# Second layer by token pairs, banks emptied by ScalarE, and longer pauses in a four-block kernel on one Trainium2 core

## The chip, the cores and the metric

The kernel runs on 1 core of one Trainium2 chip. The metric is the device time of one execution in microseconds (us). Engines are named as in the profile: PE is TensorE's matmul, PEld its weight load, DVE is VectorE, ACT is ScalarE, POOL is GpSimd, SP is SyncE. A line such as L1104 is a line of the kernel before the change.

## What is computed

The input is x, 8 batches of 512 tokens of 256 features, in float32. Four blocks follow each other, each with a layer norm ahead of it and a residual add behind it:

```
x = x + attn_a(layernorm(x))     # 16 heads; softmax attention of the 307 "sparsest" queries
x = x + ffn(layernorm(x))        # 16 blocks of 64 hidden units, the 4 likeliest are kept
x = x + attn_b(layernorm(x))     # gated linear attention, then a SwiGLU layer
x = x + ffn(layernorm(x))        # the same FFN and weights again
```

`ffn` takes softmax(x @ router_w.T + router_b), keeps the top 4 of 16 blocks per token, and computes relu(x @ w1.T + b1), masked by block, times w2.T, plus b2.

`attn_b` works along an axis of only 8 steps (the batches) with 16 heads of 16 features: S = a * S + k (x) v, o = q S. The output o is normalised per head over its 16 features, multiplied by silu(x @ wog.T + bog), and taken through wo. The kernel does this without a scan: for two steps i and j that are d apart it forms the products q * k, sums them per head, and multiplies v by the sum, with the decay folded into k or q.

## The kernel before

The first attention runs first, up to about 556 us. The change touches nothing of it. What follows is worked in four slices of tokens, k = 0 to 3: slice k holds the 128 tokens k of every one of the 8 batches, so 8 token tiles of 128 tokens, in two groups g of 4 tiles (512 columns).

**The products of the FFN and of SwiGLU** are made by `group`. A feature tile f (of NF = 8) is first computed for the 512 columns of a group in a PSUM bank of pool `r_h` (4 banks; two products of 128x512 in float32, each of which the profile lists as two records). ACT empties the bank (L1148, L1165), DVE multiplies by the mask or by the other half (L1149, L1167). This is an *up* unit. The *down* unit of f (L1104) takes the four token tiles through the second layer and adds them up over f in two banks of pool `r_y`, two token tiles in each. A list named `waiting` holds a down unit back until LAGS = 4 later feature tiles have been computed. After the last f, `end` (L1098) adds each bank to the residual `xres` on DVE and so frees it for the next group.

**Everything else** of a slice, meaning the router (`route`) and the linear attention (`gla`), is a Python generator that yields after each small step. `between(units, pieces, n)` lays n such pieces evenly between the units. The stages behind the first attention are, in order, `routed_ffn(0..3)`, `swiglu(0..3)` and `last_ffn(0..3)`; the pieces of `gla(k)` are laid into the stages ahead of `swiglu(k)`, and `some(g[1], 51)` takes 51 pieces of slice 1 ahead into the stage before. GLA is the number of pieces that one slice counts for. `pause(n)` yields n times and does nothing, so PE's work goes on while DVE and POOL compute. A swiglu stage has 48 units, a routed stage 32.

**The small products** share the two banks of pool `r_l` (`bank_l`): the transpositions of `to_channels` (tile chT_ps), the projections (`project`, tile proj_ps), the transpositions of the attention's output (oT_ps) and its output product (gla_y).

**One slice of `gla`** goes as follows. Two halves m of 8 heads are handled one after the other by `heads(m)`. First come 8 projections, one per batch, each into one bank: ACT copies key, query and value out (L1243), DVE adds the bias bog to the gate's 128 columns (L1244). ACT then takes the Silu of the whole gate (L1290). Six steps of `weighed` follow with pauses between: a one-element copy on POOL (`hold`, L1085) makes a step wait for the newest FFN result, then DVE forms products (L1256), sums them (L1258) and multiplies by v (L1266); POOL multiplies keys by the decay (L1297) and adds results up (L1283, L1303). Then ACT squares the output (L1333), POOL multiplies it by the gate (L1334) and DVE sums the squares (L1335). After both halves ACT takes the root of the variances (L1342), DVE the reciprocal (L1343) and the multiplication of o[m] (L1346); PE transposes o (L1355), and ACT copies the transposed output (L1356).

**The order on an engine** is not the order of the code. The framework plans the queue of each engine when the program is built, by its own costs and by the order in the code among what it takes to be ready. Each engine then works its queue strictly in order.

Of the kernel before, what the change touches and what calls it, by code (L numbers as in the profile page):

```python
# [15 lines left out]
ALU = mybir.AluOpType  # L16
# [3 lines left out]
P = 128  # L20
NB = 8
# [4 lines left out]
NC2 = D // P  # L26
# [3 lines left out]
NF = DFF // P  # L30
# [14 lines left out]
def block_kernel(ctx: ExitStack, tc: tile.TileContext, t: dict, out: bass.AP):  # L45
    nc = tc.nc
# [64 lines left out]
    with ExitStack() as outer:  # L111
# [75 lines left out]
        with ExitStack() as inner:  # L187
# [554 lines left out]
            for n in range(len(steps) + LAG + 1):  # L742
# [3 lines left out]
                batch, i = divmod(n - LEAD, 16)  # L746
# [91 lines left out]
        with tc.tile_pool(name="a_tail", bufs=2) as tail:  # L838
# [5 lines left out]
            last = outC[5][0:1, 1, 0:1]  # L844
# [54 lines left out]
    def bank_y(name):  # L899
        return ps_y.tile([P, 512], F32, tag="y", name=name)  # L900

    def bank_l(name):
        return ps_l.tile([P, 512], F32, tag="l", name=name)
# [15 lines left out]
    def tokens(k, b, n=2):  # L919
        return xres[:, b : b + n, k, :]  # L920

    def pairs(y):
        return y.rearrange("p (b d) -> p b d", d=D)
# [24 lines left out]
    def to_channels(rows, dst, scale):  # L948

        for c in range(NC2):  # L950
            ps = bank_l("chT_ps")
            for i in range(G4):
                nc.tensor.transpose(ps[:, bass.ts(i, P)], rows[i][:, bass.ts(c, P)], ident)
            if scale is not None:
                nc.scalar.activation(dst[:, c, :], ps, AF.Copy, scale=scale[:, c : c + 1])
            elif c == 0:
                nc.vector.tensor_copy(dst[:, c, :], ps)
            else:
                nc.scalar.copy(dst[:, c, :], ps)
            yield  # L960
# [122 lines left out]
    def hold(dst):  # L1083

        nc.gpsimd.tensor_copy(dst, newest[0])  # L1085
# [4 lines left out]
    def group(k, g, ups, w, last=False):  # L1090


        h, y = [], []

        def end(i, n):
            b = G4 * g + i
            x = tokens(k, b, n)
            nc.vector.tensor_tensor(x, x, pairs(y[i // 2])[:, i % 2 : i % 2 + n], ALU.add)  # L1098
            newest[0] = xres[0:1, b, k, 0:1]
            if last:  # L1100
                nc.sync.dma_start(out=out_v[:, b : b + n, k, :], in_=x)

        def add(f, i):
            nc.tensor.matmul(  # L1104
                y[i // 2][:, bass.ts(i % 2, D)], h[f][:, bass.ts(i, P)], w[:, f, :],
                start=(f == 0 and i % 2 == 0), stop=(f == NF - 1 and i % 2 == 1),
                skip_group_check=True,
            )

        def down(f):  # L1110
            if f == 0:
                y.extend(bank_y("y_ps") for _ in range(2))
            if last and k == 3 and g == 1 and f >= NF - 2:
                if f == NF - 1:
                    for i in range(4):
                        for e in (f - 1, f):
                            add(e, i)
                        end(i, 1)
                return
            for i in range(4):  # L1120
                add(f, i)
            if f == NF - 1:
                for i in (0, 2):
                    end(i, 2)

        units = []
        for f in range(NF):
            units += [functools.partial(up, h, g, f) for up in ups]
            waiting.append(functools.partial(down, f))
            if len(waiting) > LAGS:  # L1130
                units.append(waiting.pop(0))
        return units
# [41 lines left out]
    def heads_of(x, axis="n"):  # L1174
        return x.rearrange(f"p {axis} (h d) -> p ({axis} h) d", d=DH)

    def gla(k):
# [18 lines left out]
        ps = bank_l("gh_ps")[:, 0 : 2 * P]  # L1196
# [14 lines left out]
        for us in ((1, 2, 3), (0,)):  # L1211
            ps = [bank_l("al_ps") for u in us]
# [21 lines left out]
        def project(made, gate, m, b):  # L1234

            ps = bank_l("proj_ps")
            for c in range(NC2):
                nc.tensor.matmul(  # L1238
                    ps, rT[b // G4][:, c, bass.ts(b % G4, P)], q_w[:, c, m],
                    start=(c == 0), stop=(c == NC2 - 1),  # L1240
                )
            half = ps.rearrange("p (x n) -> p x n", n=P)
            nc.scalar.copy(made[:, :, b, :], half[:, 0:3, :])  # L1243
            nc.vector.tensor_tensor(gate[:, b, :], half[:, 3, :], bog[:, m, :], ALU.add)  # L1244

        def weighed(parts):

# [28 lines left out]
        def heads(m):  # L1276


            def fours(x):
                return x.rearrange("p (u i) n -> p u i n", i=G4)  # L1280

            def add(dst, src):
                nc.gpsimd.tensor_tensor(dst, dst, src, ALU.add)  # L1283

            made = rest.tile([P, 3, NB, P], F32, tag="made", name="made")
            gate = rest.tile([P, NB, P], F32, tag="gate", name="gate", bufs=2)
            for b in range(NB):
                project(made, gate, m, b)
                yield
            nc.scalar.activation(gate, gate, AF.Silu)  # L1290
            key, q, v = (fours(made[:, i]) for i in range(3))
            a, out = fours(al[:, :, bass.ts(m, P)]), fours(o[m])

            def near(d):
                n = G4 - d
                if d > 0:
                    nc.gpsimd.tensor_tensor(  # L1297
                        key[:, :, 0:n, :], key[:, :, 0:n, :], a[:, :, d:, :], ALU.mult
                    )
                return q[:, :, d:, :], key[:, :, 0:n, :], v[:, :, 0:n, :]  # L1300

            pr = weighed([near(0)])[0]
            nc.gpsimd.tensor_copy(out, pr)  # L1303
            yield from pause(5)
            pr = weighed([near(1)])[0]
            add(out[:, :, 1:, :], pr)
            yield from pause(4)
            for d in (2, 3):
                pr = weighed([near(d)])[0]
                add(out[:, :, d:, :], pr)  # L1310
                yield from pause(4 - d // 3)
            nc.gpsimd.tensor_tensor(q[:, 1, 0, :], q[:, 1, 0, :], a[:, 1, 0, :], ALU.mult)
            nc.gpsimd.tensor_tensor(
                q[:, 1, 1:, :], q[:, 1, 1:, :], far[:, :, bass.ts(m, P)], ALU.mult
            )
            every = [P, 2, G4, P]
            for s in (0, 2):
                pr = weighed([(
                    q[:, 1].unsqueeze(1).to_broadcast(every),
                    key[:, 0, s : s + 2, :].unsqueeze(2).to_broadcast(every),  # L1320
                    v[:, 0, s : s + 2, :].unsqueeze(2).to_broadcast(every),
                )])[0]
                if s == 0:
                    for i in range(2):
                        add(out[:, 1], pr[:, i])
                else:

                    nc.vector.tensor_tensor(pr[:, 0], pr[:, 0], pr[:, 1], ALU.add)
                    nc.vector.tensor_tensor(out[:, 1], out[:, 1], pr[:, 0], ALU.add)
                yield from pause(5 + s)  # L1330
            sq = rest.tile([P, NB, P], F32, tag="pr", name="sq", bufs=2)
            hold(sq[0:1, 0, 0:1])
            nc.scalar.activation(sq, o[m], AF.Square)  # L1333
            nc.gpsimd.tensor_tensor(o[m], o[m], gate, ALU.mult)  # L1334
            nc.vector.tensor_reduce(var[:, m, :], heads_of(sq), AX.X, ALU.add)  # L1335
            yield
# [4 lines left out]
            yield from heads(m)  # L1341
        nc.scalar.activation(var, var, AF.Sqrt, bias=eps, scale=1.0 / DH)  # L1342
        nc.vector.reciprocal(var, var)  # L1343
        oT = rest.tile([P, 2, NC2, 512], F32, tag="made", name="oT")
        for m in range(NC2):
            nc.vector.tensor_tensor(  # L1346
                heads_of(o[m]), heads_of(o[m]),
                var[:, m, :].unsqueeze(2).to_broadcast([P, NB * P // DH, DH]), ALU.mult,
            )
            yield from pause(1 + m)  # L1350
        for g in range(2):
            for m in range(NC2):
                ps = bank_l("oT_ps")
                for i in range(G4):
                    nc.tensor.transpose(ps[:, bass.ts(i, P)], o[m][:, G4 * g + i, :], ident)  # L1355
                nc.scalar.copy(oT[:, g, m, :], ps)  # L1356
                yield
# [42 lines left out]
        ready["z", k] = zT  # L1400


    GLA = 97

    def chain(*gens):
        return itertools.chain(*gens)
# [1 line left out]
    def pause(n):  # L1408

        for _ in range(n):  # L1410
            yield
# [11 lines left out]
    bog = wpool.tile([P, NC2, P], F32, name="bog")  # L1423
# [7 lines left out]
    ps = bank_l("bog_ps")[:, 0:D]  # L1431
    nc.tensor.matmul(ps, ones, turned, start=True, stop=True)
    nc.vector.tensor_copy(bog.rearrange("p m n -> p (m n)"), ps)
    g = [gla(k) for k in range(4)]
# [17 lines left out]
    )  # L1452
    between(routed_ffn(3, (1, 3)), chain(g[0], some(g[1], 51)), GLA - 91 + 51)
    between(swiglu(0), chain(g[1], some(g[2], 36)), GLA - 51 + 36)
    between(swiglu(1), chain(g[2], some(g[3], 26)), GLA - 36 + 26)
    between(swiglu(2), chain(g[3], route(0, (2, 0))), GLA - 26 + ROUTE)
    resting.close()
# [107 lines left out]
```

## Time and profile before

| | |
|---|---|
| time, median of 3 runs | 1571.51 us (1569.48 to 1574.36) |
| profiled execution, its own time | 1567.76 us |
| its span, first to last instruction | 1566.0 us |
| mean granted TensorE clock | 0.983 |
| DVE busy, share of the span | 985.5 us, 63% |
| ACT busy | 735.3 us, 47% |
| POOL busy | 451.9 us, 29% |

A group's line reads: kernel line, engine, operation, output<-inputs, shape, count | busy us, mean ns | idle time of the engine just before it and what ended that. A line of waits reads: engine and line that waited <- engine and line that ended the wait: us in total, times, longest us. A line of windows gives, for a stretch from A to B in us, its length, then busy us and number of instructions of PE, PEld, DVE, ACT and POOL, then the granted clock of PE, the DMA share and GB/s. A line of the timeline gives start and duration in us, engine, line, operation, output<-input and count, and in brackets the idle time of the engine before it and what ended it. Neighbouring instructions of one line are merged.

### The profile page before, as it was taken

Reading aid. Unit: us, or ns where it says so; the run is one execution under the profiler, and the core shown is the slowest. Engines: PE = TensorE matmul, PEld = TensorE weight load, DVE = VectorE, ACT = ScalarE, POOL = GpSimd, SP = SyncE. Lnnn points to the kernel's source line nnn. Section 1 sums busy time; section 2 is a strip of 40 time slices with the busy share of each in tenths; the row PEclk is TensorE's granted clock in tenths of the full one; section 3 lists DMA queues with packets and bytes.
Section 4 is the critical chain, followed back from the end, with each engine's and each line's share of the span. In section 5 each row is a group of like instructions: output and inputs, shape, how many; then the busy total and the mean of one; then the engine's idle time right before and its main releaser. Section 6 shows DMA issues by size and latency. Waiting matters only on the chain.

```text
span 1566.0 us, 21950 instructions
## 1 busy us (share of the span) xinstructions
PE 1519.2 (97%) x8110; PEld 882.8 (56%) x8110; DVE 985.5 (63%) x2047; ACT 735.3 (47%) x1341; POOL 451.9 (29%) x547
## 2 busy tenths in 40 slices
PE   6899999999999999999999999999999999999999
PEld 2444444444444376655565556555555656788887
DVE  5878776776778983636773674457375733476654
ACT  3457777777766843452336216323613363232221
POOL 4743443433320151133341443224233221010000
PEclk8879999999999999999999999999999999999999
DMA  5302111111120051100000000000000010011110
GB/s 185 133 2 79 46 43 69 46 53 49 43 76 3 3 175 28 28 14 14 2 26 0 1 1 1 0 0 1 1 0 1 0 28 1 1 41 41 41 41 27
DMA packets 38571, 52.68 MB, mean 34 GB/s; under 512 B 9084, under 2 KB 22596, under 8 KB 38464
## 3 DMA queue, kind: packets, MB, share of 16 engines
q1 hardware_dynamic: 37664, 50.09, 9.8%
q8 instruction: 64, 1.05, 0.3%
q10 hardware_dynamic: 800, 1.18, 0.2%
q14 instruction: 43, 0.35, 0.1%
HBM read 21.24 MB, written 4.33 MB: 16 GB/s over the span
## 4 chain that ended last, share of the span: by engine, by line
PE 73%; DVE 14%; POOL 5%; ACT 4%; issue 2%; DMA 2%; SPq 1%; POOLq 0%; ACTq 0%; DVEq 0%
PE y_ps L1104 15%; PE s L612 10%; PE av L634 8%; PE swi_ps L1160 7%; PE proj_ps L1238 6%; PE s L586 4%; PE h_ps L1496 4%; PE h_ps L1143 4%; DVE pr L1266 3%; DVE pr L1256 3%; DVE w L1258 2%; PE hd_ps L1496 2%; PE gla_y L1363 2%; PE q_ps L444 2%; PE k_ps L444 2%
## 5 line engine op out<-in xcount | busy, mean ns | idle before, releaser
L592 DVE TENSOR_REDUCE mx<-s 128x1 f32<-128x512 f32 x512 | 325.3, 684 | 115.9 <-PE s L586 115.2
L619 ACT ACTIVATE e<-s 128x512 f32<-128x512 f32 x512 | 276.1, 600 | 127.2 <-PE s L612 121.0
L1104 PE MATMUL y_ps<-w,h 128*128 128x256 f32 x1024 | 246.3, 382 | 5.6 <-DVE xres L1098 5.5
L1104 PEld LDWEIGHTS y_ps<-w,h 128*128 128x128 f32 x1024 | 193.2, 191 | 59.4 <-issue 24.3
L634 PE MATMUL av<-e,va 128*32 128x512 f32 (+1 forms) x1216 | 148.4, 558 | 2.1 <-ACT st L644 2.0
L586 PE MATMUL s<-km,qh 32*128 32x512 f32 x512 | 136.9, 509 | 7.6 <-DMA ql<-half 6.0
L612 PE MATMUL s<-qh,km 32*128 32x512 f32 x512 | 140.1, 508 | 0.4 <-ACT e L619 0.3
L1104 PE MATMUL y_ps<-w_down,h 128*128 128x256 f32 x512 | 123.6, 380 | 0.0
L1143 PE MATMUL h_ps<-xnT,w 128*128 128x512 f32 x256 | 121.7, 595 | 0.0
L1160 PE MATMUL swi_ps<-zT,w_gate 128*128 128x512 f32 x256 | 121.7, 593 | 0.0
L1160 PE MATMUL swi_ps<-zT,w_up 128*128 128x512 f32 x256 | 121.7, 593 | 0.0
L1238 PE MATMUL proj_ps<-q_w,rT 128*128 128x512 f32 x256 | 116.8, 598 | 3.7 <-DVE gate L1244 3.6
L1104 PEld LDWEIGHTS y_ps<-w_down,h 128*128 128x128 f32 x512 | 95.8, 190 | 35.0 <-issue 24.8
L612 PE MATMUL s<-ql,km 32*128 32x512 f32 x512 | 112.4, 408 | 0.0
L586 PEld LDWEIGHTS s<-km,qh 32*128 32x128 f32 x512 | 54.9, 187 | 98.8 <-DVE mx L592 66.2
L586 PE MATMUL s<-km,ql 32*128 32x512 f32 x512 | 110.4, 411 | 0.0
L612 PE MATMUL s<-tops,takes 4*128 4x512 f32 x512 | 110.4, 402 | 0.0
L1165 ACT ACTIVATE h<-swi_ps 128x512 f32<-128x512 f32 x64 | 38.0, 594 | 151.0 <-PE swi_ps L1160 150.9
L1502 ACT ACTIVATE h<-hd_ps,b 128x512 f32<-128x512 f32 x64 | 43.9, 685 | 125.9 <-PE hd_ps L1496 125.7
L1148 ACT ACTIVATE h<-h_ps,b 128x512 f32<-128x512 f32 x64 | 43.9, 686 | 123.8 <-PE h_ps L1143 123.7
L612 PEld LDWEIGHTS s<-qh,km 32*128 32x128 f32 x512 | 57.0, 187 | 75.8 <-ACT e L619 52.6
L1004 POOL TENSOR_TENSOR xres<-xres,b 128x512 f32<-128x512 f32 x32 | 41.1, 1300 | 201.4 <-ACT row L943 146.3
(247 smaller groups left out, 2549.8 us busy)
## 6 DMA issues: line engine op xcount, KB each, us to landing
mk<-md SPq DMA_DIRECT2D x32, 256.0 KB
qh<-half SPq DMA_DIRECT2D x63, 128.0 KB
ql<-half SPq DMA_DIRECT2D x63, 128.0 KB
km<-half SPq DMA_DIRECT2D x63, 128.0 KB
xres<-in_L_attn_a_x SPq DMA_DIRECT2D x7, 512.0 KB
out<-xres SPq DMA_DIRECT2D x14, 256.0 KB
w<-in_f_w1T SPq DMA_DIRECT2D x1, 1024.0 KB
w<-in_f_w2T SPq DMA_DIRECT2D x1, 1024.0 KB
```

The source lines that it names most:

```text
L444: nc.tensor.matmul(ps, w[:, c, bass.ts(m, P)], x[:, c, :], start=(c == 0), stop=(c == NC2 - 1),)
L586: nc.tensor.matmul(s, (qh, ql)[i].bitcast(HALF)[rows, e, bass.ts(k, P)], km.bitcast(HALF)[rows, e, :], start=(i == 0), stop=(i == 1),)
L592: nc.vector.tensor_reduce(mx[:, b % 2, m, e, r : r + 1], s, AX.X, ALU.max)
L612: nc.tensor.matmul(s, keys.bitcast(HALF), queries.bitcast(HALF), start=(i == 0), stop=(i == 2),)
L619: nc.scalar.activation(ex, s, AF.Exp, scale=1.0 / DH**0.5)
L634: nc.tensor.matmul(av[32 * j : 32 * j + 32, queries], va[:, 8 * kt + 4 * m + j, DH * e : DH * e + 2 * DH], es[j][:, queries], start=(kt == ...
L1104: nc.tensor.matmul(y[i // 2][:, bass.ts(i % 2, D)], h[f][:, bass.ts(i, P)], w[:, f, :], start=(f == 0 and i % 2 == 0), stop=(f == NF - 1 a ...
L1143: nc.tensor.matmul(ps, w1[:, c, bass.ts(f, P)], xT[g][:, c, :], start=(c == 0), stop=(c == NC2 - 1),)
L1160: nc.tensor.matmul(ps, w[:, c, bass.ts(f, P)], zT[g][:, c, :], start=(c == 0), stop=(c == NC2 - 1),)
L1238: nc.tensor.matmul(ps, rT[b // G4][:, c, bass.ts(b % G4, P)], q_w[:, c, m], start=(c == 0), stop=(c == NC2 - 1),)
L1256: nc.vector.tensor_tensor(views[-1], q, key, ALU.mult)
L1496: nc.tensor.matmul(yd if i == 2 else y, w1s[i][:, c, bass.ts(f, P)].bitcast(HALF), xs[n][i][:, c, :].bitcast(HALF), start=(c == 0 and i != 1),
```

## The change

It has four parts.

1. In `heads`' norm: two pauses ahead of the multiplication of o[0], two instead of one behind it (two as before behind that of o[1]); the transpositions of o go over m outside and g inside. GLA goes from 97 to 100 accordingly.
2. In `project`, ACT copies the gate's columns out of the bank, and the bias is added afterwards by one POOL instruction over all 8 batches, ahead of the Silu.
3. In `group`, the down unit of the last feature tile but one does nothing, and that of the last does both, by pairs of token tiles: four products for tiles 0 and 1, `end` of their bank, four for tiles 2 and 3, `end` of theirs. In the very last group this was already done by single tiles, and stays so.
4. In `to_channels`, where no scale is given (the router's use), ACT makes both copies; DVE made the first.

```diff
@@ to_channels
                 nc.scalar.activation(dst[:, c, :], ps, AF.Copy, scale=scale[:, c : c + 1])
-            elif c == 0:
-                nc.vector.tensor_copy(dst[:, c, :], ps)
             else:
                 nc.scalar.copy(dst[:, c, :], ps)
@@ group: down
-            if last and k == 3 and g == 1 and f >= NF - 2:
-                if f == NF - 1:
-                    for i in range(4):
-                        for e in (f - 1, f):
-                            add(e, i)
-                        end(i, 1)
-                return
-            for i in range(4):
-                add(f, i)
-            if f == NF - 1:
-                for i in (0, 2):
-                    end(i, 2)
+            if f < NF - 2:
+                for i in range(4):
+                    add(f, i)
+            elif f == NF - 1:
+                n = 1 if last and k == 3 and g == 1 else 2
+                for i in range(0, 4, n):
+                    for e in (f - 1, f):
+                        for j in range(i, i + n):
+                            add(e, j)
+                    end(i, n)
@@ gla: project
             nc.scalar.copy(made[:, :, b, :], half[:, 0:3, :])
-            nc.vector.tensor_tensor(gate[:, b, :], half[:, 3, :], bog[:, m, :], ALU.add)
+            nc.scalar.copy(gate[:, b, :], half[:, 3, :])
@@ gla: heads, ahead of the Silu
+            nc.gpsimd.tensor_tensor(
+                gate, gate, bog[:, m, :].unsqueeze(1).to_broadcast([P, NB, P]), ALU.add
+            )
             nc.scalar.activation(gate, gate, AF.Silu)
@@ gla: norm of the heads
         nc.vector.reciprocal(var, var)
+        yield from pause(2)
...
-            yield from pause(1 + m)
-        for g in range(2):
-            for m in range(NC2):
+            yield from pause(2)
+        for m in range(NC2):
+            for g in range(2):
                 ps = bank_l("oT_ps")
@@
-    GLA = 97
+    GLA = 100
```

## The prediction

> **What bounds the kernel now.** I read first the page's busy times: is there an engine that has no room left?
>
> ```profile
> PE 1519.2 (97%) x8110; PEld 882.8 (56%) x8110; DVE 985.5 (63%) x2047; ACT 735.3 (47%) x1341; POOL 451.9 (29%) x547
> ```
>
> PE (TensorE) is busy 97% of the span, so only time in which PE stands still can be won; work moved among DVE, ACT and POOL is worth what it does to PE's waits. All edits lie behind the first attention, so next I asked who PE waits for from 575 us on.
>
> ```profile
> PE oT_ps L1355 <- DVE o L1346: 5.8, 5, 2.5
> PE y_ps L1104 <- DVE xres L1098: 5.5, 3, 2.7
> PE proj_ps L1238 <- DVE gate L1244: 3.6, 2, 2.3
> PE chT_ps L953 <- DVE xnT L957: 2.4, 1, 2.4
> PE mT_ps L1066 <- DVE taken L1059: 1.0, 3, 0.5
> ```
>
> That is 18.3 us, all of it for DVE, which is in arrears there. The edits touch the first four: 17.3 us. Third, the windows around two of these waits show a second loss.
>
> ```profile
> 720.00:740.00 20.00, 17.69 (x46) 9.10 (x46) 10.56 (x15) 4.51 (x8) 5.10 (x4) 0.91 0.10 27
> 868.00:884.00 16.00, 13.33 (x42) 8.71 (x41) 12.65 (x25) 2.06 (x3) 8.36 (x10) 0.89 0.00 0
> ```
>
> The granted clock (third figure from the end) falls to 0.91 and 0.89: 0.09 x 20 and 0.11 x 16, some 1.8 us each, are lost at half rate after a wait. The ceiling is 17.3 + 3.6 = 20.9 us. Last, the timeline shows why DVE is late: first the steps behind the wait at 874 us, then how a head's first step starts.
>
> ```profile
> 869.54 0.69 DVE L1256 TENSOR_TENSOR pr<-made 128x512 f32<-128x512 f32 x1 [1.82 <-POOL pr L1085]
> ...
> 873.43 0.17 POOL L1085 COPY pr<-h 1x1 f32<-1x1 f32 x1
> 873.64 0.43 DVE L1256 TENSOR_TENSOR pr<-made 128x256 f32<-128x256 f32 x1 [1.28 <-POOL pr L1085]
> ...
> 876.08 1.27 DVE L1098 TENSOR_TENSOR xres<-xres,y_ps 128x512 f32<-128x512 f32 x2
> 876.80 3.41 PE L1104 MATMUL y_ps<-w,h 128*128 128x256 f32 x8 [2.67 <-DVE xres L1098]
> ```
> ```profile
> 694.41 0.17 POOL L1085 COPY pr<-h 1x1 f32<-1x1 f32 x1 [13.77 <-DVE h L1149]
> ...
> 695.16 0.29 DVE L1244 TENSOR_TENSOR gate<-proj_ps,bog 128x128 f32<-128x128 f32 x1 [0.82 <-ACT made L1243]
> 695.37 1.22 DVE L1256 TENSOR_TENSOR pr<-made 128x1024 f32<-128x1024 f32 x1
> ...
> 697.03 1.82 POOL L1297 TENSOR_TENSOR made<-made,al 128x768 f32<-128x768 f32 x1 [2.45 <-DVE pr L1256]
> ...
> 718.87 3.79 POOL L1283 TENSOR_TENSOR o<-o,pr 128x512 f32<-128x512 f32 x2
> 719.24 2.28 DVE L1256 TENSOR_TENSOR pr<-made 128x1024 f32<-128x1024 f32 x1
> ```
>
> A head is a chain of DVE and POOL steps, and a late link makes everything behind it late. L1297 of the second step also runs at 697.03, before L1303 of the first (700.39): the framework plans each queue, so code order isn't queue order. And the same 1024-element DVE product takes 1.22 us alone but 2.28 us beside a POOL add: 1.06 us of contention.
>
> **Part 1, pauses and oT order.** A slice's generator makes 86 steps before its first oT transposition, 89 after. Slice 1 has done 51 in the stage before, so the transposition falls in piece 36 of 82, then 39 of 85; over 48 units that is unit 21.07, then 22.02. What counts is the distance to the last head's first step, with which the late chain begins: piece 4 of 82, then of 85, unit 2.34, then 2.26. Since the other pieces become denser, three pauses buy only 1.03 unit. Slices 2 and 3 give the same (28.1 to 28.8 against 10.5 to 10.1; 36.1 to 36.6 against 17.2 to 16.6). A unit is 1.72 us of PE (four records 0.429 us apart), so 1.77 us. The waits are 0.33 us in slice 0, 2.48 in slice 1, 1.29 in slice 2, 1.22 in slice 3 and 0.51 there for o[1], which goes too because both groups of o[0] are now transposed first. Sum 0.33 + 1.77 + 1.29 + 1.22 + 0.51 = 5.1 us, between 2 (DVE slips along) and 5.8 (all).
>
> **Part 2, the gate.** Removed from DVE: 64 x 0.292 = 18.7 us (L1244). Added on ACT: 64 copies of 128x128 from PSUM at 0.266 (row L1021), 17.0 us. Added on POOL: 8 adds like L1334's (128x1024, 2.358), 18.9 us. ACT is busy 262 of 687 us in this stretch and the copies lie between products 1.72 us long, so they are hidden; without that cover each would hold a bank 0.27 us longer. What it gains: at 729.27 the gate's add began 0.85 us after the ACT copy of the same bank ended (728.47), queued behind L1335; an ACT copy follows at once and ends about 0.8 us sooner. At 1177.50 the same comparison gives 0.5. Sum 1.3 us of 3.6; the rest is ACT itself being late behind the square L1333. Half rate followed the gaps of 2.31 and 2.67 us, but not those of 2.36 (763) and 2.48 (944), where the windows give a clock of 1.00. If the wait at 727 shrinks, its stretch of 1.8 us may therefore go: I take half, 0.9. The Trainium skill ("TensorE: Matmul & The Clock Gate", HAM oscillation) names PE gaps beyond about 3.4 us as what cools the array; by that rule nothing would be won here and the sum would be 0.9 less, but the two shorter gaps speak against it.
>
> What it costs: the Silu on ACT now waits for POOL. Behind it stand the FFN's activations, and who waits for those is the second layer four units later, 13.8 us: hidden, 2.6 us a head if not. The POOL add runs beside the head's first DVE product: 1.06 us of contention, as at 719 us. The Trainium skill ("GPSIMD Engine Reference", Key points) warns of it where DVE reads two SBUF inputs, without a price; it speaks against this edit. How much reaches PE? In a head the hold L1085 stands in POOL's queue behind the add of the step before (869.34 behind an L1283 that ends at 869.38), and DVE waits for the hold: a chain that makes up nothing. So I let it arrive in full where a wait of PE lies behind the head: 1.06 at 704, 874, 944, 1176 and 1229 us, and 0.7 at 1088, where the hold came 1.7 us after the last gate. At the transpositions the spare of part 1 takes some: slice 2 keeps 1.29 - 1.77 + 0.7 = 0.22, slice 3 1.22 - 1.77 + 1.06 = 0.51, slice 1 all of 1.06. With 3 x 1.06 at 704, 874 and 1176: 5.0 us lost, between 0 (the planner moves it) and 8.5 (all eight heads).
>
> **Part 3, second layer by pairs.** No instruction is added. The first bank's last product moves four products ahead of the second's instead of two: 0.86 us more room for L1098. In the waits at 704 and 874 the bank had long been ready and DVE came late, so this gives nothing unless the planner finds an earlier slot; at 786 I count it: 0.9 us. Ends: all of 5.5 plus the half-rate 1.8, or below nothing, -1.7, if the emptied unit (1.72 us of PE gone ahead) makes an activation late. PE shows no wait of h_ps or swi_ps, so I cost that at zero.
>
> **Part 4, the router's copies.** 16 x 0.690 us leave DVE, 16 x 0.566 come to ACT. At 763 PE waited 2.4 us for one that DVE began only at 765.47, while ACT's sister copy was done at 760.77. But ACT then stood 5.15 us before the root L73. If the copies queue behind that, the second ends at about 768.5 instead of 766.7. Between +2.4 and -1.8; I take +1.2, half, since the first copy is the one PE waited for.
>
> **Sum.** 5.1 + 1.3 + 0.9 - 5.0 + 0.9 + 1.2 = 4.4 us. From the profiled execution's 1567.76 (span 1566.0 and 1.8 around it) that gives 1563.4. The median of the runs, 1571.51, lies 3.75 above that execution; against the median the sum gives 1567.1 us.
>
> **Rivals.** *Slower: the gate's add ahead of the hold on POOL.* In six of eight heads the one-element copy L1085 runs before the last gate is ready, but at 694.41 and 856.72 by only 1.04 us, and in two heads (750, 1054) after it. If POOL takes the add first, DVE's first product waits for copy, add and hold: 0.27 + 2.36 + 0.17 + 0.1 = 2.9 us, 1.84 more than counted. In six heads that is 11.0, and one more stretch at half rate 1.8: 4.4 - 12.8 = -8.4, so 1580. It decides from 4.4 / 6 = 0.73 us more delay per head; beyond that the change loses. For it: the margin is smallest in just the heads that are late. Against it: the hold needs nothing of the gate.
>
> *Everything goes.* The planner puts L1098 into DVE's idle time (1.28 us before 873.64), contention falls where DVE has room, and the four waits vanish: 20.9 us at most, 14 likely, so 1557.5. For it: idle time lies in the right place. Against it: DVE did not use it before.
>
> *Nothing to measure.* DVE stays as late and the waits move to the next product: 2 us gained to 4 lost, about 1572. For it: only the last link of each wait differs, not the chain before it.
>
> **How the numbers follow.** Chances: forecast 0.42, everything goes 0.19, nothing 0.17, slower 0.22. A measurement here tells 0.3%, 4.7 us, from no change. The forecast's own range is 1563 to 1571, and 0.20 of its 0.42 lies beyond 4.7 us. Faster 0.20 + 0.19 = 0.39; within 0.22 + 0.15 = 0.37; slower 0.22 + 0.02 = 0.24. The range reaches from 1555 (short of the ceiling, 0.07 below it) to 1579 (near the slower rival's price, 0.13 above it).
>
> **What would show it.** Right: PE's list has no L957 and hardly any L1355; the gate's wait names ACT and is shorter; the first L1256 product of a head takes about 2.3 us beside the new POOL add. The forecast is wrong if L1098's row grows past 8 us (slower), if it vanishes (everything), or if a wait for h_ps, swi_ps or an ACT line takes the place of DVE's.

## The result: 0.8% slower, and the profile after

The changed kernel takes 1584.97 us (median; 1579.27 to 1592.55), the kernel before 1571.12 beside it: a ratio of 1.0083, with a 95% interval of 1.0057 to 1.0110, or 13.0 us more (9.0 to 17.3). The forecast of 1567.1 has the wrong sign, and the time lies beyond the upper end of the range.

The profiled execution of the changed kernel took 1586.71 us. Its page begins with the engines' busy times:

```profile
PE 1531.3 (97%) x8110; PEld 888.4 (56%) x8110; DVE 967.1 (61%) x1967; ACT 756.2 (48%) x1423; POOL 475.0 (30%) x555
```

The work moved as intended: DVE has 18.4 us less, ACT 20.9 and POOL 23.1 more. But PE's waits from 575 us on, in the changed kernel's line numbers, did not shrink:

```profile
PE oT_ps L1355 <- DVE o L1346: 9.1, 3, 4.4
PE proj_ps L1234 <- ACT gate L1240: 8.7, 5, 2.4
PE y_ps L1102 <- DVE xres L1096: 3.4, 3, 1.5
PE lg_ps L1013 <- ACT xnT L957: 1.7, 1, 1.7
```

With three small lines the sum is 24.0 us; it was 18.3. The wait for the second layer's bank shrank from 5.5 to 3.4, and that for chT_ps is gone. The transpositions' wait grew from 5.8 to 9.1, that of the projections from 3.6 to 8.7, and the latter now names an ACT line. The window around the longest wait shows what follows it:

```profile
952.00:968.00 16.00, 11.56 (x42) 8.50 (x41) 5.80 (x7) 9.36 (x12) 2.31 (x1) 0.79 0.00 0
```

PE stands still for 4.44 us, and then the granted clock of the window is 0.79. From 575 us on the clock's records give 13.7 us at half rate (a granted clock of 0.5) after, 6.8 before; half of that is lost, so 3.4 us more. Waits and clock together explain 9.1 us.

The two profiled executions differ by 18.95 us, but not all of that is the change. Ahead of 575 us, in code that is the same, the clock's records show 64.9 us at half rate after and 47.8 before, 8.5 us of loss that the change has no part in. In the eighteen profiles below, all with the same code there, this half-rate time lies between 34 and 72 us. So below I compare waits and clock from 575 us on, and take the size of an effect from the ratios.

Why did the waits grow? A head's start shows it. First the kernel before, at its fifth head:

```profile
1005.87 1.22 DVE L1256 TENSOR_TENSOR pr<-made 128x1024 f32<-128x1024 f32 x1
...
1007.24 1.81 POOL L1297 TENSOR_TENSOR made<-made,al 128x768 f32<-128x768 f32 x1 [6.32 <-DVE pr L1256]
1008.38 2.08 DVE L1266 TENSOR_TENSOR pr<-made,w 128x512 f32<-128x512 f32 x2
...
1010.60 1.04 POOL L1303 COPY o<-pr 128x1024 f32<-128x1024 f32 x1 [0.68 <-DVE pr L1266]
...
1011.58 0.17 POOL L1085 COPY pr<-h 1x1 f32<-1x1 f32 x1
1011.78 0.96 DVE L1256 TENSOR_TENSOR pr<-made 128x768 f32<-128x768 f32 x1 [0.72 <-POOL pr L1085]
```

Then the changed kernel, the same head:

```profile
1019.66 1.22 DVE L1252 TENSOR_TENSOR pr<-made 128x1024 f32<-128x1024 f32 x1 [6.70 <-ACT made L1239]
1019.81 3.30 POOL L1286 TENSOR_TENSOR gate<-gate,bog 128x1024 f32<-128x1024 f32 x1 [6.61 <-ACT gate L1240]
...
1022.18 3.70 DVE L1262 TENSOR_TENSOR pr<-made,w 128x512 f32<-128x512 f32 x2
1023.06 2.27 POOL L1296 TENSOR_TENSOR made<-made,al 128x768 f32<-128x768 f32 x1
...
1026.14 1.03 POOL L1302 COPY o<-pr 128x1024 f32<-128x1024 f32 x1
...
1027.12 0.17 POOL L1083 COPY pr<-h 1x1 f32<-1x1 f32 x1
1027.33 0.96 DVE L1252 TENSOR_TENSOR pr<-made 128x768 f32<-128x768 f32 x1 [0.85 <-POOL pr L1083]
```

POOL's idle time ahead of the key multiplication is now filled by the bias add, which takes 3.30 us. The key multiplication starts only at its end, 3.4 us after the first product began (1.37 before). DVE's multiplication by v, two instructions in the line of 3.70 us, so meets both: the first of the two takes 1.48 us beside the end of the add, the second 2.30 beside the key multiplication. Before they took 1.22 and 0.94, together 2.08. The copy into o needs that multiplication and stands behind POOL's queue; the hold stands behind the copy. From the end of the last projection's ACT copy to the second step's first product it was 6.15 us (1005.63 to 1011.78); it is 7.77 (1019.56 to 1027.33). The 1.62 us between them is as much as DVE's multiplication was drawn out by.

### The profile page after: what moved, and what is told of

It is laid out like the page before. It is cut to its first block, busy times and chain, and to the rows that moved or that the text cites. A ratio compares the mean times of both kernels' runs of the same rounds, so it can differ in the third digit from the quotient of the medians.

```text
span 1584.9 us, 22011 instructions
## 1 busy us (share of the span) xinstructions
PE 1531.3 (97%) x8110; PEld 888.4 (56%) x8110; DVE 967.1 (61%) x1967; ACT 756.2 (48%) x1423; POOL 475.0 (30%) x555
## 4 chain that ended last, share of the span: by engine, by line
PE 72%; DVE 12%; POOL 6%; issue 4%; ACT 3%; DMA 2%; SPq 1%; POOLq 0%; ACTq 0%; DVEq 0%
PE y_ps L1102 15%; PE s L612 9%; PE swi_ps L1156 8%; PE av L634 7%; PE proj_ps L1234 6%; PE s L586 4%; PE h_ps L1496 4%; PE h_ps L1139 4%; DVE pr L1252 3%; DVE pr L1262 2%; DVE w L1254 2%; PE hd_ps L1496 2%; PE chT_ps L953 2%; PE gla_y L1363 2%; POOL o L1279 2%
## 5 line engine op out<-in xcount | busy, mean ns | idle before, releaser
L1163 DVE TENSOR_TENSOR h<-h,swi_ps 128x512 f32<-128x512 f32 x64 | 43.6, 682 | 153.3 <-PE swi_ps L1156 117.0
L1145 DVE TENSOR_TENSOR h<-h,mk 128x512 f32<-128x512 f32 x64 | 50.6, 801 | 102.0 <-ACT h L1144 95.0
```

Source lines behind the costliest of these rows:

```text
L1145: nc.vector.tensor_tensor(hf, hf, mk[g][:, f, :], ALU.mult)
```

## The experiments

The theory: the one large POOL add, standing in the way at each head's start, makes the chain late, and PE's waits grow by as much; the rest of the change moves waits about. The rivals: the pauses or the pairs cost the time; ACT's longer queue does, or its Silu, which now waits for the add; POOL's or ACT's added work as such does. All ratios are to the kernel before, run beside each kernel, with 95% intervals. The second table column is the sum of PE's waits from 575 us on in each profile, the third the loss at half rate there (half of the time that the clock's records show).

| kernel | ratio | waits, us | half rate, us |
|---|---|---|---|
| before | 1 | 18.3 | 3.4 |
| the whole change | 1.0083 (1.0057 to 1.0110) | 24.0 | 6.8 |
| only_gate (part 2) | 1.0056 (1.0031 to 1.0081) | 25.5 | 13.7 |
| only_pauses (part 1) | 1.0012 (0.9991 to 1.0033) | 20.0 | 3.4 |
| only_pairs (part 3) | 1.0014 (0.9990 to 1.0037) | 21.6 | 6.8 |
| only_copies (part 4) | 0.9979 (0.9954 to 1.0003) | 16.6 | 5.1 |
| all_but_gate (1, 3, 4) | 1.0008 (0.9983 to 1.0034) | 17.3 | 5.1 |
| gate_no_add | 0.9974 (0.9953 to 0.9994) | 14.7 | 3.4 |
| gate_late | 1.0063 (1.0041 to 1.0085) | 26.0 | 10.2 |
| after_late | 1.0069 (1.0043 to 1.0095) | 23.5 | 11.9 |
| gate_held | 1.0069 (1.0043 to 1.0094) | 24.9 | 10.2 |
| after_held | 1.0041 (1.0014 to 1.0069) | 21.8 | 10.2 |
| copies_held | 1.0028 (1.0002 to 1.0055) | 22.2 | 10.2 |
| long_pause | 1.0031 (1.0008 to 1.0055) | 21.6 | 10.7 |
| gate_dve | 1.0011 (0.9987 to 1.0035) | 19.0 | 5.1 |
| gate_each | 0.9976 (0.9955 to 0.9997) | 16.3 | 3.4 |
| copies_each | 0.9967 (0.9949 to 0.9984) | 15.6 | 3.4 |
| after_each | 1.0007 (0.9985 to 1.0029) | 15.8 | 8.5 |

**Each part alone.** Part 2, the gate, by its lines of the diff (the Silu stays where it was, behind the add):

> Kernel of before with part 2 alone (gate's columns copied by ACT, one POOL add over all batches ahead of the Silu). Theory, the add in the chain: in the changed kernel each head's second step begins 1.6 to 2.6 us later after the last projection, because L1297 and the hold stand behind the POOL add. So this part alone makes the kernel slower by 6 to 12 us, with PE waiting for o (L1346) and for the gate's bank. Rival, density: the added pauses are the cause, and this part alone costs at most 2 us. Rival, ACT: the loss comes from the banks being held longer by ACT's second copy; then the waits of proj_ps grow here as well, but those of oT_ps stay near 5.8 us.

Measured 1.0056: of the four parts the only one that is clearly different from no change, 8.8 of the 13.0 us. Its waits:

```profile
PE oT_ps L1358 <- DVE o L1349: 8.7, 3, 4.1
PE y_ps L1104 <- DVE xres L1098: 8.2, 3, 4.3
PE chT_ps L953 <- DVE xnT L957: 4.5, 1, 4.5
```

All three lie behind the late chain of a head. That y_ps exceeds 8 us is the sign that the prediction had named for a slower kernel. The Silu does begin late on ACT (in the fifth head 3.57 us after the last projection's copy, 0.36 before), but from 575 us on no wait of PE in this run names h_ps, swi_ps or the lines that empty them, so this delay did not reach PE there.

Part 1, the pauses and the order of the transpositions, by its lines of the diff:

> Kernel of before with part 1 alone (three more pauses at the heads' norm, transpositions of o by halves first). Theory, the add in the chain: the pauses do what they were costed at in part, the waits of oT_ps fall from 5.8 to 1 to 3 us, and the kernel gains 2 to 5 us. Rival, density: pieces laid 4 to 5% denser bring the next half's projections and the second layer to the late chain earlier; oT_ps loses its waits but proj_ps and y_ps gain 5 us or more, and the kernel is 3 to 8 us slower.

Measured 1.0012, no difference that can be told, and neither expectation came as put. In its waits the transpositions gained almost nothing, and the projections doubled (they were 3.6):

```profile
PE proj_ps L1238 <- DVE gate L1244: 7.0, 5, 2.3
PE oT_ps L1356 <- DVE o L1347: 5.4, 4, 2.5
```

Part 3, the pairs of token tiles, by its lines of the diff:

> Kernel of before with part 3 alone (last two feature tiles' second layer by pairs). Theory: between 0 and 4 us gained, the waits of y_ps (5.5 us) fall to 2 to 4. Rival, the emptied unit: PE runs 1.72 us ahead into products whose activations are not done; then waits for h_ps or swi_ps appear and the kernel is 2 to 5 us slower.

Measured 1.0014. The wait for the bank fell from 5.5 to 3.5 us (the one near 788 us, 1.44, is gone, that near 707 shrank by 1.0, that near 878 stayed), and others took more than that back: the transpositions rose from 5.8 to 7.8, the projections from 3.6 to 6.2.

```profile
PE oT_ps L1353 <- DVE o L1344: 7.8, 4, 2.4
PE proj_ps L1236 <- DVE gate L1242: 6.2, 3, 3.1
PE y_ps L1104 <- DVE xres L1098: 3.5, 3, 2.7
```

Part 4, the router's copies, by its lines of the diff:

> Kernel of before with part 4 alone (the router's first copy on ACT). Theory: within 2 us of before, the wait of chT_ps (2.4 us) goes and one for ACT of up to 2 us takes its place. Rival: ACT's copies queue behind the root L73, which waits for DVE; then PE waits 3 us or more for xnT L957/L959, and the kernel is 3 us or more slower.

Measured 0.9979, probably a small gain, but the interval reaches 1.0003. The wait of 2.4 us for DVE became one of 2.0 for ACT.

**Which half of part 2?** gate_no_add leaves out the bias of the gate altogether; the ACT copies stay:

```diff
-            nc.gpsimd.tensor_tensor(gate, gate, bog..., ALU.add)
```

> The kernel with part 2 alone, but without the POOL add: the bias of the gate is left out of the computation, ACT still copies the gate's columns. Theory, the add in the chain: the loss of part 2 alone (0.56%, 8.8 us) goes, the time is within 3 us of before or up to 4 us below it, and a head's second step begins about 6 us after its last projection's copy instead of 7.6 to 8.6. Rival, ACT: the second copy holds the banks and blocks ACT's queue; the time stays 5 us or more above before.

Measured 0.9974: the copies gain 4.1 us (0.9 to 7.4), and the add costs the difference to only_gate, 0.82% or 12.9 us (some 8 to 18, from both intervals). The head's start is back at 5.95 to 6.3 us in six heads (7.75 to 8.23 in the same six in only_gate).

```profile
PE oT_ps L1355 <- DVE o L1346: 5.5, 5, 2.3
PE y_ps L1104 <- DVE xres L1098: 4.8, 3, 2.5
PE chT_ps L953 <- DVE xnT L957: 2.3, 1, 2.3
```

**Can it be moved by its place in the code?** In gate_late, add and Silu stand behind the last weighed step:

```diff
                     nc.vector.tensor_tensor(out[:, 1], out[:, 1], pr[:, 0], ALU.add)
+                    nc.gpsimd.tensor_tensor(gate, gate, bog..., ALU.add)
+                    nc.scalar.activation(gate, gate, AF.Silu)
```

> The kernel with part 2 alone, but the POOL add and the Silu placed behind the last weighed step of the head, where POOL stood idle for about 5 us before the copy ahead of the square (L1085 at 1034.40). Theory, the place of the add: same work on the same engines, but off the front of the chain: within 4 us of before, at least 5 us faster than part 2 alone. Rival, contention: the add costs DVE 1.06 us a head wherever it lies, and the loss stays above 5 us.

Measured 1.0063. The planner put the first add at 693.72 us, where only_gate has it at 693.70: only_gate once more, and it tells nothing new of a later add. after_late, the whole change with the same edit, went the same way:

> The changed kernel with the POOL add and the Silu behind the last weighed step. Theory, the place of the add: some 9 us faster than the changed kernel, so within 5 us of before. Rival, density: the pauses and pairs keep it 7 us or more above before.

Measured 1.0069. The parts without the gate came to no difference, as their single ratios let expect (all_but_gate: parts 1, 3 and 4 of the diff as they stand):

> The changed kernel with DVE's gate add as before (parts 1, 3 and 4). Alone these gave +0.12%, +0.14% and -0.21%. Theory, parts add up: within 4 us of before. Rival, they work together: with copies and banks relieved, the pauses pay and the kernel is 5 us or more faster; or the denser pieces and the emptied unit meet and it is 5 us or more slower.

Measured 1.0008.

**A later add, made late by its data.** In gate_held the add writes another tile, into which POOL first copies one element of the last weighed step's product:

```diff
@@ weighed(parts, then=None), after the first product
+                if then is not None:
+                    then(views[-1][0:1, 0, 0, 0:1])
@@ heads; given as `then` to the last weighed step
+            def open_gate(late):
+                nc.gpsimd.tensor_copy(opened[0:1, 0, 0:1], late)
+                nc.gpsimd.tensor_tensor(opened, gate, bog..., ALU.add)
+                nc.scalar.activation(opened, opened, AF.Silu)
...
-            nc.gpsimd.tensor_tensor(o[m], o[m], gate, ALU.mult)
+            nc.gpsimd.tensor_tensor(o[m], o[m], opened, ALU.mult)
```

> Part 2 alone, with the POOL add made to wait: it writes a tile of its own, whose first element POOL copies from the first product of the head's last weighed step; the add and the Silu can so not start before it. (Moved in the code alone, the add had stayed at the head's front: 693.72 as against 693.70.) Theory, the place of the add: a head's second step begins about 6.0 us after the last projection's copy again, the square ends 30 to 32 us after it, and the time is within 4 us of before, 5 us or more below part 2 alone. Rival, POOL's and DVE's shared time: the add costs as much wherever it lies, and the time stays 5 us or more above before.

Measured 1.0069, a miss. Now the add did move, and the head's start was back at 5.95 to 6.3 us in six heads. But the delay came back at the other end of the chain, first before, then here:

```profile
1031.66 1.29 DVE L1266 TENSOR_TENSOR pr<-made,w 128x512 f32<-128x512 f32 x2
```
```profile
1042.77 2.36 POOL L1322 TENSOR_TENSOR opened<-gate,bog 128x1024 f32<-128x1024 f32 x1
1043.81 2.47 DVE L1268 TENSOR_TENSOR pr<-made,w 128x512 f32<-128x512 f32 x2
```

The last step's two multiplications take 2.47 us beside the add; in the kernel before, with POOL idle, the same two took 1.29 (at 1031.66). Against gate_no_add the square ends 1.2 to 2.6 us later in all eight heads. So the start is not the only bad place: at both ends of a head a DVE product with two inputs from SBUF stands on the chain. The same with the whole change, and with part 4 alone:

> The whole change with the POOL add held back in the same way. Theory: as the change without its gate part (+0.08%), within 4 us of before. Rival, density: pauses and pairs bring the next half's projections ahead of the chain, and with the add's contention the kernel stays 6 us or more above before.

> Parts 2 and 4 alone, with the POOL add held back. The router's copies on ACT alone gave -0.21%, the gate's columns on ACT without the add -0.26%. Theory: the two savings of DVE time add up, less the held add's contention: 2 to 7 us below before. Rival: the held add lies in POOL's way at the head's end, and the time is at before or up to 5 us above.

Measured 1.0041 and 1.0028: both still slower, where their rivals had put them (6.4 and 4.4 us above before).

**Does the bias belong on POOL at all?** gate_dve leaves the large add where it is and gives it to DVE:

```diff
-            nc.gpsimd.tensor_tensor(gate, gate, bog..., ALU.add)
+            nc.vector.tensor_tensor(gate, gate, bog..., ALU.add)
```

> Part 2 alone, but with the one large add on DVE instead of POOL, at the same place. Theory, meeting the chain: DVE's add of 128x1024 takes about 1.2 us and delays the chain by that or less, with no contention: +2 to +6 us. Rival, POOL's sharing of SBUF with DVE is the whole cost: within 2 us of before.

Measured 1.0011: 0.45% (some 0.1 to 0.8) less than only_gate, from the engine alone. On DVE the add takes 1.22 us instead of 3.3, and the second step starts after 5.7 to 7.2 us in six heads. It gives back about what the ACT copies gain. The 1.7 us above before lie in the rival's range, just under the theory's, and the interval (-2.0 to +5.5) holds both; this run does not tell the two apart.

gate_each leaves it on POOL, but adds each batch's 128 columns as soon as ACT has copied them, while the projections still run:

```diff
+            nc.gpsimd.tensor_tensor(gate[:, b, :], gate[:, b, :], bog[:, m, :], ALU.add)
```

> Part 2 alone, but the bias is added on POOL batch by batch, 128x128 at a time, behind each of ACT's copies. The same 64 x 128 columns pass through POOL, but seven eighths of it while the projections run, where DVE and POOL wait for PE; only the last add (0.46 us alone by L1312's row) meets the chain. Theory, meeting the chain is what costs: the second step begins about 6.0 us after the last projection's copy, the square as without the add (29 to 31 us), and the time is 2 to 5 us below before, like the kernel without the add (-0.26%). Rival, POOL's time as such: 64 adds with their fixed time are more POOL work, and the time stays 5 us or more above before.

Measured 0.9976: as good as without the add, though POOL is busier than in only_gate (487.3 us against 477.5).

```profile
693.61 0.46 POOL L1245 TENSOR_TENSOR gate<-gate,bog 128x128 f32<-128x128 f32 x1 [2.99 <-ACT gate L1244]
...
698.62 1.23 DVE L1257 TENSOR_TENSOR pr<-made 128x1024 f32<-128x1024 f32 x1 [0.89 <-ACT made L1243]
...
698.76 1.40 POOL L1245 TENSOR_TENSOR gate<-gate,bog 128x128 f32<-128x128 f32 x1 [0.79 <-ACT gate L1244]
```

The small adds lie in POOL's idle time, as at 693.61; only the last of a head stands beside DVE's first product and is drawn out from 0.46 to 1.40 us, but ends at 700.16, 0.3 us after the product, and the key multiplication follows at 700.12, at its end. The second step starts after 6.15 to 6.5 us in six heads. This settles the question: neither POOL's work as such nor ACT's queue costs the time, but one long POOL add that ends after the chain has begun.

**The better version, and the whole change with it.** copies_each is gate_each with part 4; after_each is all four parts with the small adds:

> As gate_each, with part 4 (the router's copies on ACT, alone -0.21%). Theory: the two add up, 4 to 9 us below before. Rival: PE's waits move to ACT's lines, and it is no faster than either alone (2 to 4 us below).

> The whole change with the bias added batch by batch on POOL. Theory: the changed kernel's loss was part 2's one large add; with it gone the time is that of the change without its gate part (+0.08%) less some 4 us: 0 to 6 us below before. Rival, pauses and pairs cost by themselves: 3 us or more above before.

copies_each measured 0.9967 (0.9949 to 0.9984), 1567.22 us: faster than both kernels. after_each measured 1.0007, where 0 to 6 us below before had been expected: the small adds take nearly all of the loss out of the whole change, 0.76%, and what parts 1 and 3 add to copies_each is a loss of 0.4% (some 0.1 to 0.7).

**Do pauses move the transpositions?** long_pause has 14 pauses behind o[1] instead of two:

```diff
-            yield from pause(1 + m)
+            yield from pause(1 + 13 * m)
...
-    GLA = 97
+    GLA = 109
```

> The kernel of before with 14 instead of 2 pauses behind the multiplication of o[1], and GLA 109. In all kernels so far, with three pauses more or without, PE's first transposition of o stands behind the same amount of FFN products (137, 214, 288.5 to 289 and 361 to 361.5, counted in fours of PE's records). Theory, the planner places it by the time at which it takes o to be ready, and a pause only moves the earliest place: by code the places become about 217, 289 and 362, so slice 1's wait (2.5 us) goes, slice 2's (1.3 us) stays and slice 3's shrinks by less than 1 us. Simple theory of the prediction: each pause is worth its share of a unit, and all three waits go. Either way the other pieces are 10 to 15% denser, so proj_ps and y_ps may wait 3 to 10 us more: the time is 0 to 10 us above before.

Measured 1.0031. I counted the units of SwiGLU's and the FFN's products on PE ahead of each slice's first transposition: 137, 214, 289 and 361.5 in the kernel before; 137, 214, 288.5 and 361 in the changed kernel; 142, 217, 289 and 362 here. Three pauses moved none of them later; twelve moved slices 0 and 1 by 5 and 3 units, the others by half at most. The places of slices 1 to 3 are those that the theory had given; but the waits of the transpositions are gone altogether, in slices 2 and 3 too, where the place hardly changed, and there the theory missed. In these two the chain came sooner: the projections of the slice's second half, counted in the same units, begin at 256 and 326, before at 257 and 329. The projections and the second layer wait in their stead:

```profile
PE proj_ps L1238 <- DVE gate L1244: 10.8, 4, 3.5
PE y_ps L1104 <- DVE xres L1098: 6.9, 4, 3.8
```

## Why the prediction was wrong, step by step

| step | predicted, us | measured, us |
|---|---|---|
| part 1, pauses and order | -5.1 | +1.9 (-1.4 to +5.2) |
| part 2, ACT copies and the half-rate stretch | -2.2 | -4.1 (-7.4 to -0.9) |
| part 2, the POOL add | +5.0 | +12.9 (some +8 to +18) |
| part 3, pairs | -0.9 | +2.2 (-1.6 to +5.8) |
| part 4, copies | -1.2 | -3.3 (-7.2 to +0.5) |
| sum | -4.4 | +9.6; the whole change +13.0 |

Two steps failed: the price of the POOL add, 5.0 us counted and 12.9 measured, and the gain of the pauses, 5.1 us counted and 1.9 lost. The measured figures are the ratios times 1571.5 us; the add's is the difference of only_gate and gate_no_add. The 3.4 us between the sum and the whole lie within the intervals.

- **"The POOL add runs beside the head's first DVE product: 1.06 us of contention."** The mechanism was right, its place and size were not. Near 719 the POOL add had begun first, and 1.06 us was what DVE then had to wait. In the changed kernel the first product kept its 1.22 us in seven heads; in four of them it ran beside the add and began first, and it was the add that became longer, 3.30 instead of 2.36. The delay came two steps later, from the end of the add and from the key multiplication that stands behind it in POOL's queue, at DVE's multiplication by v: 1.62 us in the head above, over half as much again as 1.06. Only in the fourth head did the add begin first, and there the product took 3.22. I had costed the moved instruction beside its first neighbour only, and not asked what stands behind it in its own queue. Against the kernel without the add, the head's end (the square) comes 1.7 to 2.2 us later in six heads of only_gate, 4.9 in the second and 0.4 in the sixth. The Trainium skill ("GPSIMD Engine Reference", Key points) speaks of contention with DVE instructions that read two inputs from SBUF; the rows agree in that DVE's sum of the first product, with one input, kept its 1.22 us beside the add.
- **"I let it arrive in full where a wait of PE lies behind the head."** This held. PE's waits are 10.8 us longer in only_gate than without the add. The five that I had charged with 1.06 us grew by 1.8 to 1.9 each (now near 706, 880, 952, 1187 and 1241 us), the one charged with 0.7 by 0.4, and the wait for chT_ps near 766, which I had not charged, by 2.2. What I left out as well is half rate after longer waits: 13.7 us lost against 3.4 in those two executions. Waits and half rate would make 21 us, more than the 12.9 of the ratios, so a part of the half rate belongs to these executions and not to the add.
- **"Three pauses buy 1.77 us", and the 5.1 us in all.** This step failed by nearly as much as the add did, 7.0 us against 7.9. I computed the transposition's place from the generator's pieces, but the planner places it by what it takes to be ready, the theory that gave long_pause's places; with three pauses it stands where it stood in slices 0 and 1, and half a unit earlier in the others. They do move projections: in only_pauses those of the third and seventh head begin 2.5 and 3.5 units later, those of the sixth and eighth one unit earlier, and PE's waits for the gate's bank rose from 3.6 to 7.0 us. The place on PE is also the same, to half a unit, with the add (137.5, 214, 289 and 361.5 in only_gate): the plan leaves the add no room there, so the chain's delay turns into waiting.
- **Part 3, "at 786 I count it: 0.9".** The wait for the bank shrank by 2.0 us, 1.44 of it at the place counted and 1.0 near 707 (the prediction's 704), where I had counted nothing; a new one of 0.4 came near 882. So the mechanism was right. That the waits then move on to the transpositions and projections was the third rival's thought, which I had not applied here.
- **Part 2's gain and part 4.** Both had the right sign and were set low, within their intervals. The wait for the gate's bank fell by 2.5 us in gate_no_add (3.6 to 1.1), where 1.3 was counted (from 728.47 to 729.27 it is 0.80 us, not 0.85; the sum had used 0.8). The stretch at half rate near 730 went, as the 0.9 us supposed, but another came near 950, so the loss at half rate stayed 3.4 us.
- **The rival "slower".** Its price of 1580 and its point of 0.73 us more delay per head were nearest to the truth. Its mechanism was only half right: in five heads of the changed kernel the hold still ran ahead of the add. In the sixth and eighth the first product did wait for add and hold and began 2.75 us after the last copy, where the rival had put 2.9. In most of the others it was the work behind the add, key multiplication, copy and next hold, that came late. I had argued against it that the hold needs nothing of the gate; it need not, since a queue in order is enough.
- **The signs.** "An ACT line takes the place of DVE's" came true at proj_ps, and an L1098 row past 8 us in only_gate. Of the signs of being right, the gate's wait names ACT but is longer, the transpositions' wait grew, and the first product took about 2.3 us in no head.

What stays open is how parts 1 and 3 lose their 0.4% together in after_each. In only_pauses two heads start their second step later than before (the third after 8.09 us instead of 6.49, the eighth after 8.17 instead of 6.14) and the sixth sooner (6.94 instead of 8.34), and after_each has the same three; its second head also starts late (9.84, 8.35 before), as in only_pairs (9.40). No run took these apart. The sum of waits in after_each, 15.8 us, is like that of copies_each, 15.6; the profile of after_each has 5.1 us more loss at half rate, but that varies between executions.

## What to carry to other kernels

An instruction that moves to an engine with idle time is costed with everything behind it in that engine's queue up to the next link of the chain, and each of those pieces beside its new neighbours; about 2 us in each of six heads were here more than all the gains. Cut moved work small and let it run as its inputs come: the same additions cost 12.9 us in one piece per head and nothing in eight. Where a planner orders the queues, pauses and places in the code are requests: three pauses left the transpositions where they were, twelve moved them by 5 units at most, and the add moved only when its data made it wait. A wait that is won at one product can return at the next.

## What the runs showed of the hardware

- Where the bias add on POOL met a DVE instruction with two inputs from SBUF in the rows shown, the one that began first kept its time and the other waited. The 128x1024 add took 3.30 us at 1019.81, beside DVE's first product, which had begun 0.15 us sooner and kept 1.22. In the fourth head of the changed kernel the add began first:

```profile
917.81 2.34 POOL L1286 TENSOR_TENSOR gate<-gate,bog 128x1024 f32<-128x1024 f32 x1 [3.09 <-ACT gate L1240]
918.02 3.22 DVE L1252 TENSOR_TENSOR pr<-made 128x1024 f32<-128x1024 f32 x1 [3.61 <-ACT gate L1240]
```

At 1042.77 in gate_held it began first too, kept 2.36, and DVE's two multiplications went from 1.29 to 2.47. In all these cases and in gate_each's 1.40 (0.46 alone) the later one ended 0.13 to 0.15 us before the end of the first plus its own time alone. So the price of a meeting is no fixed 1.06 us: it is what is left of the instruction that began first.
- Half rate does not follow a gap's length alone. In the profiles of before, after, only_gate, gate_no_add, gate_each, copies_each, long_pause and gate_held, a stretch of 3.41 or 6.83 us at half rate followed 19 of 30 PE gaps between 1.9 and 3.1 us, and all 7 over 3.5 us; a gap of 2.61 us was followed by it in gate_each and not in the changed kernel. The Trainium skill ("TensorE: Matmul & The Clock Gate", HAM oscillation) names gaps beyond about 3.4 us; the shorter ones measured here speak against that as a limit. The same page (Part 1) has a window of that length that runs freely; the steps of 3.41 us agree with such a window, but no run here was made to show it.
